# Three chunks per scatter matmul, and the clear of the accumulators on ACT, in a graph attention kernel

## The chip, the cores and the metric

The kernel runs on one core of a Trainium2 chip. The metric is the device time of one execution in microseconds. Three timed executions of the kernel before took 4207.81, 4209.71 and 4210.2 us; the median is 4209.71 us. Engines are named as the profile names them: PE is TensorE's matmul, PEld its weight load, DVE is VectorE, ACT is ScalarE, POOL is GpSimd, SP is SyncE, which here only issues transfers.

## The reference

A graph with 12500 nodes and 412500 edges, sorted by target node. The layer normalises the node features, projects them, weighs every edge by a softmax over the edges of its target, and adds up the source rows:

```python
h = relu(layernorm(x)) @ W_node.T            # (12500, 4 heads, 32)
e = edge_features @ W_edge.T                 # (412500, 4, 32)
att = leaky_relu(sum(concat([h[src], h[tgt], e]) * a, -1), 0.2)
m = maximum(segment_max(att, tgt), 0)
ex = exp(att - m[tgt])
denom = segment_sum(ex, tgt) + (E - deg)[:, None] * exp(-m)
out = x + segment_sum((ex / denom[tgt])[..., None] * h[src], tgt)
```

## The kernel before, in words

**Preparation.** All nodes are normalised and projected first. The 98 blocks of 128 nodes go in groups of up to nine blocks, and these in units of three: measure takes the statistics (bn_stats, on DVE), root and deviate turn them into scale and shift (ACT, DVE), normalize writes hn (two blocks on ACT, one on DVE), turn transposes it on PE into PSUM (pt) and lets DVE write the rectified copy hT, project multiplies by the weights, keep_rows copies to SBUF on ACT, and write stores a finished group into the table in HBM. The loop runs a counter k: iteration k projects unit k, normalizes and turns unit k + 2 and measures unit k + 6. The order in the code is the order on each engine. The accumulator acc (128 x 392 x 35 numbers) is cleared by a GpSimd memset before the loop (L329). After the loop the extents of the chunks are found (L220 to L223).

**Main loop.** A chunk is 896 edges, seven tiles of 128; a batch is eight chunks, and there are 58 batches, the last with five chunks of which the last holds three tiles. Iteration b of the loop works on two batches at once. For batch b + 1 load fetches the edge features and gather fetches one table row per edge: one indirect DMA per tile, 56 for a full batch, all issued by GpSimd (L481). The gathered rows (hs) have two buffers, so gather of batch b + 1 may start only when the scatter of batch b - 1 has read the same buffer. That is done by a gate: ACT copies a column of the finished sums into a tile sums (L579), and GpSimd copies it into gate (L479) before its first gather. For batch b, weigh computes the attention on DVE and ACT, scatter multiplies the rows by it on DVE (L562) and adds them up per target on PE (L569), and collect copies the sums from PSUM to a tile r on ACT (L591; in the last batch every other copy is made by DVE, L589). begin makes the logits z of batch b + 1 (L499, L502, on PE) and its memberships hot (L518, on DVE). After every second batch, and after each of the last two, merge combines the chunks (L598 to L629) and adds them to acc (L638); finish divides a group of blocks, adds x and writes the output.

**Scatter.** The 896 edges of a chunk reach at most 32 target rows, so a tile's membership is a 128 x 32 matrix of zeros and ones. It is the stationary operand; the 128 x 140 weighted rows (four heads of 35) are the moving one. G is 4: chunk q accumulates in column group q mod 4 of the PE array and the same partitions of PSUM, with a tile position of its own. Two chunks are multiplied and added at a time, their tiles in turns. All is in float32, and each matmul of the program is two PE instructions. Memberships are in tiles of 14 edge tiles, four buffers in turn.

Of the kernel before, what the change touches and what calls it, by code (L numbers as in the profile page):

```python
# [9 lines left out]
F32 = mybir.dt.float32  # L10
# [3 lines left out]
OP = mybir.AluOpType  # L14
# [3 lines left out]
P = 128  # L18
# [18 lines left out]
MB = 2  # L37
MC = MB * CB
W = 32
G = P // W  # L40
NB = -(-N // P)
NQ = NB * (P // W)
GB = 7
# [19 lines left out]
def merges():  # L63

    pairs = [(b, b + MB - 1) for b in range(0, NBT - MB, MB)]
    return pairs + [(b, b) for b in range(len(pairs) * MB, NBT)]


def parts():
# [20 lines left out]
def kernel(  # L90
# [57 lines left out]
    twb = const.tile([P, 2, 2, R], F32, name="twb")  # L148
    nc.gpsimd.memset(twb, 0.0)
    gate = const.tile([P, 1], F32, name="gate")  # L150
    sums = const.tile([P, 1], F32, name="sums")
    carry_m = const.tile([P, 1], F32, name="carry_m")
    nc.gpsimd.memset(carry_m, 0.0)
    carry = const.tile([P, AW - 1], F32, name="carry")
# [13 lines left out]
    with (  # L168
# [124 lines left out]
        def turn(u):  # L293
            pt = pps.tile([P, XS, P], F32, name="pt")
            for i in range(u.m):
                nc.tensor.transpose(pt[:, i, :], u.hn[:, i, :], ident)
            u.hT = p2.tile([P, XS, P], F32, name="hT", bufs=3)
            nc.vector.tensor_scalar(u.hT[:, :u.m, :], pt[:, :u.m, :], 0.0, None, op0=OP.max)

        def project(u):  # L300
            u.ph = pps.tile([P, XS, ROW], F32, name="ph")
# [24 lines left out]

        for _ in range(4):
            load_next()
        nc.gpsimd.memset(acc, 0.0)  # L329
        ahead = 6  # L330
        for u in units[:ahead - 2]:
            for s in rooted:
# [19 lines left out]
        while k < len(units):  # L352
            for s in rooted:
                deviate(s)
            rooted.clear()
            if 0 <= k:
                project(units[k])
            if k + 2 < len(units):
                normalize(units[k + 2])
            for s in measured:  # L360
                root(s)
            measured.clear()
            if full:
                write(full)
            if k + 2 < len(units):
                turn(units[k + 2])
                u = units[k + 2]
                if u is u.s.units[-1]:
                    load_next()
            full = keep_rows(units[k]) if 0 <= k else None  # L370
            if k + ahead < len(units):
                measure(units[k + ahead])
            if k == 4:
                early = [index(b) for b in range(2)]
                load_extents()
            if k % 4 == 0 and 0 <= k // 4 - 4 < NG:
                find_rise(k // 4 - 4)
            k += 1
# [64 lines left out]
    em_ps = bank[:, T * R + W:]  # L443
    nc.scalar.copy(rows_ps, riota)

    class Batch:
        pass

# [27 lines left out]
    def gather(s, sums=None):  # L476

        if sums is not None:
            nc.gpsimd.tensor_copy(gate, sums)  # L479
        for i in s.tiles:  # L480
            nc.gpsimd.indirect_dma_start(  # L481
                out=s.hs[:, i, :], out_offset=None, in_=table[:, :],
                in_offset=bass.IndirectOffsetOnAxis(ap=s.src[:, i:i + 1], axis=0))
# [6 lines left out]
    def begin(s):  # L490

        for k in range(2):
            pair = 2 * s.b + k
            nc.vector.tensor_scalar(s.mem[:, k, :], s.mem[:, k, :].bitcast(I32), nid[:, pair:pair + 1], None,  # L494
                                    op0=OP.is_equal)
        s.z = ps.tile([R, CE], F32, name="z")
        for part in (slice(0, HALF), slice(HALF, CE)):
            for j in range(SB):
                nc.tensor.matmul(s.z[:, part], wa3[:, j, :], s.eft[:, j, part], start=(j == 0), stop=False)  # L499
        for part in (slice(0, HALF), slice(HALF, CE)):  # L500
            for k in range(2):
# [10 lines left out]
        s.hot = []  # L512
        for j in range(SB):
            sc = s.b * SB + j
            if not tiles_of(sc):
                continue
            hot = work.tile([P, CT, W], F32, name="hot", bufs=4)
            nc.vector.tensor_tensor(hot, rows_ps[:, None, :].to_broadcast([P, CT, W]),  # L518
                                    key[:, j * CT:(j + 1) * CT, None].to_broadcast([P, CT, W]),
                                    op=OP.is_equal)  # L520
            s.hot.append(hot)

    def weigh(s):

# [27 lines left out]

    def scatter(s):

        s.pa = ps.tile([P, CB // G, H * AW], F32, name="pa", bufs=2)
        by_chunk = s.hs[:, :, :EROW].rearrange("p (q t) (h k) -> p q t h k", t=T, h=H)
        for j in range(SB):
            tiles = list(enumerate(tiles_of(s.b * SB + j)))
            for c, n in tiles:
                q = 2 * j + c  # L560
                rows = by_chunk[:, q, :n, :, :HB]
                nc.vector.tensor_tensor(  # L562
                    rows, rows, ex_ps[:, :n, q * H:(q + 1) * H, None].to_broadcast([P, n, H, HB]), op=OP.mult)
            for i in range(T):
                for c, n in tiles:
                    if i < n:
                        q = 2 * j + c
                        g = q % G
                        nc.tensor.matmul(s.pa[g * W:(g + 1) * W, q // G, :], s.hot[j][:, c * T + i, :],  # L569
                                         s.hs[:, q * T + i, :EROW],  # L570
                                         start=(i == 0), stop=(i == n - 1), tile_position=(0, g * W))

    merged = {}

    def collect(s, first, n):


        if s.b + 2 < NBT:
            nc.scalar.copy(sums, s.pa[:, CB // G - 1, 0:1])  # L579
        if s.b == first:  # L580
            r = work.tile([P, AW * (MC + 1)], F32, name="r")
            merged["r"] = r[:, :AW * (n + 1)].rearrange("p (d c) -> p d c", d=AW)
        at = 1 + (s.b - first) * CB
        for g in range(min(s.chunks, G)):
            to = merged["r"][:, :, at + g:at + s.chunks:G]
            for h in range(H):
                what = s.pa[g * W:(g + 1) * W, :-(-(s.chunks - g) // G), h * AW:(h + 1) * AW]
                if s.b == NBT - 1 and h % 2:
                    nc.vector.tensor_copy(to[h * W:(h + 1) * W, :, :], what.rearrange("p c d -> p d c"))  # L589
                else:  # L590
                    nc.scalar.copy(to[h * W:(h + 1) * W, :, :], what.rearrange("p c d -> p d c"))  # L591

    def merge(c0, n):

# [132 lines left out]
    with tc.manual_schedule():  # L727
        for b in range(-1, NBT):
            if b == -1:
                for k in range(2):  # L730
                    batch(k).src, batch(k).dst = early[k]
                load_pen(batch(0))
            elif b + 2 < NBT:
                batch(b + 2).src, batch(b + 2).dst = index(b + 2)
            if b + 1 < NBT:
                load(batch(b + 1))
                gather(batch(b + 1), sums if b >= 1 else None)
            if b >= 0:
                s = batch(b)
                weigh(s)  # L740
                if b + 1 < NBT:
                    load_pen(batch(b + 1))
                for store in stores:
                    store()
                stores.clear()
                scatter(s)
            if b + 1 < NBT:
                begin(batch(b + 1))
            if b >= 0:
                first, last = next((i, j) for i, j in merges() if i <= b <= j)  # L750
                n = min((last + 1) * CB, NCH) - first * CB
                collect(batch(b), first, n)
                if b == last:
                    merge(first * CB, n)
# [259 lines left out]
```

## Time and profile before

| what | value |
|---|---|
| median of the timed executions | 4209.71 us |
| profiled execution, own time | 5270.07 us |
| profiled execution, span | 5268.3 us |
| TensorE clock granted, mean | 0.599 |
| POOL busy | 3102.0 us, 59% |
| DVE busy | 1776.6 us, 34% |
| PE busy | 1494.8 us, 28% |
| ACT busy | 500.8 us, 10% |
| first gather issued | 111.46 us |
| last gather issued | 5182.26 us |

The profiled execution is much longer than the timed ones, so a share of its span is not a share of the median. In a row of a group the numbers after the bar are busy time in us, the mean of one instruction in ns, and the time that the engine stood idle just before them, with what ended most of it. In a row of the waits the numbers are the sum in us, the count, and the longest. In the timeline they are start and length in us; "x8" means eight instructions drawn together.

### The profile page before, as it was taken

To read this page: it belongs to the slowest core of one execution; us is meant where nothing else is said; L and a number is where in the kernel's file an instruction comes from. 1 tells how busy PE (TensorE), PEld (TensorE's weight loads), DVE (VectorE), ACT (ScalarE), POOL (GpSimd) and SP (SyncE) were. 2 spreads that over 40 slices of the span, in tenths; PEclk is the share of its full clock that TensorE was granted. 3 is DMA by queue.
4 is the path that set the end of the run, shared out by engine and by line. 5 is a ranking of instruction groups with operands and counts; after the bars stand their busy time and mean duration, and the time that the engine had idled before them with its cause. 6 is when DMAs were issued, how large, how long until landed. Compare 5 with 4: busy or idle time off the path is not lost.

```text
span 5268.3 us, 30111 instructions
## 1 busy us (share of the span) xinstructions
PE 1494.8 (28%) x8641; PEld 736.7 (14%) x8641; DVE 1776.6 (34%) x3342; ACT 500.8 (10%) x1629; POOL 3102.0 (59%) x3338
## 2 busy tenths in 40 slices
PE   5232213322323132223232322232323223322223
PEld 4011101111111011111110111111111111111111
DVE  7132424242234142332331432423223324242235
ACT  3010101010001010100010100000101001000001
POOL 3766656556656656565566464655665656555652
PEclk7565656565656565656565655565656656555656
DMA  4332323232323232223232232332232323232321
GB/s 139 100 91 70 112 67 95 73 93 72 96 72 94 70 92 78 84 79 93 72 89 80 81 86 68 94 90 75 83 86 66 101 66 96 75 90 69 98 70 47
DMA packets 243648, 441.28 MB, mean 84 GB/s; under 512 B 93946, under 2 KB 144118, under 8 KB 243478
## 3 DMA queue, kind: packets, MB, share of 16 engines
q0 software_dynamic: 103136, 237.83, 17.7%
q1 hardware_dynamic: 127030, 194.11, 10.7%
q10 hardware_dynamic: 13312, 7.36, 0.5%
q8 instruction: 72, 1.18, 0.1%
q14 instruction: 98, 0.80, 0.0%
HBM read 423.75 MB, written 15.29 MB: 83 GB/s over the span
## 4 chain that ended last, share of the span: by engine, by line
issue 34%; POOL 22%; another core or an unknown queue 15%; PE 12%; DVE 11%; DMA 3%; ACT 2%; DVEq 0%; SPq 0%; ACTq 0%; POOLq 0%
POOL hs L481 22%; PE pa L569 10%; DVE hs L562 2%; DMA hs<-table,src 2%; ACT r L591 1%; PE z L499 1%; DVE up L539 1%; DVE m L541 1%; DMA twb<-table 1%; DVE z L535 1%; DVE acc L638 1%; ACT a L536 1%; DVE a L542 0%; ACT both L545 0%
## 5 line engine op out<-in xcount | busy, mean ns | idle before, releaser
L481 POOL DMA_INDIRECT hs<-table,src x3223 | 3064.6, 951 | 1009.4 <-issue 969.1
L569 PE MATMUL pa<-hs,hot 128*32 128x140 f32 x6446 | 875.0, 397 | 3515.6 <-issue 1754.9
L569 PEld LDWEIGHTS pa<-hs,hot 128*32 128x32 f32 x6446 | 515.1, 151 | 3896.6 <-issue 2021.8
L518 DVE TENSOR_TENSOR hot<-exr,key 128x448 f32<-128x448 f32 x231 | 140.1, 623 | 1940.3 <-remote 1193.2
L479 POOL COPY gate<-sums 128x1 f32<-128x1 f32 x56 | 10.2, 183 | 992.0 <-ACT sums L579 992.0
L562 DVE TENSOR_TENSOR hs<-hs,exr 128x924 f32<-128x924 f32 x461 | 476.8, 1102 | 0.0
L499 PE MATMUL z<-eft,wa 128*32 128x384 f32 (+1 forms) x928 | 373.6, 557 | 22.0 <-issue 22.0
L708 DVE TENSOR_TENSOR xg<-up,xg 128x448 f32<-128x448 f32 (+2 forms) x30 | 16.4, 589 | 771.4 <-remote 767.6
L579 ACT COPY sums<-pa 128x1 f32<-128x1 f32 x56 | 8.9, 159 | 2777.8 <-PE pa L569 2777.8
L591 ACT COPY r<-pa 32x70 f32<-32x70 f32 (+1 forms) x920 | 250.7, 272 | 31.8 <-PE pa L569 19.8
L536 ACT ACTIVATE a<-z 32x224 f32<-32x224 f32 x232 | 80.5, 347 | 1329.1 <-DVE z L535 1079.2
L502 PE MATMUL z<-mem,twb 128*32 128x512 f32 x464 | 186.5, 545 | 5.1 <-DMA twb<-table 5.1
L535 DVE TENSOR_TENSOR z<-z,zst 32x224 f32<-32x224 f32 x232 | 89.8, 387 | 277.4 <-PE z L502 151.4
L499 PEld LDWEIGHTS z<-eft,wa 128*32 128x32 f32 x928 | 99.9, 113 | 238.9 <-issue 234.4
L545 ACT ACTIVATE both<-a 32x224 f32<-32x224 f32 x232 | 89.9, 388 | 370.9 <-DVE a L542 257.1
L638 DVE TENSOR_TENSOR acc<-acc,a 128x70 f32 x461 | 110.0, 239 | 32.9 <-issue 16.5
L539 DVE TENSOR_TENSOR_SCAN up<-pen,z 32x896 f32<-32x896 f32 x58 | 117.0, 2017 | 2.0
L541 DVE TENSOR_TENSOR_SCAN m<-pen,up 32x896 f32<-32x896 f32 x58 | 116.4, 2007 | 2.0
L547 DVE SCALAR_TENSOR_TENSOR both<-pen,m 32x224 f32<-32x224 f32 x232 | 88.0, 380 | 17.8 <-issue 15.7
L703 PE MATMUL up<-a,ident 128*32 128x224 f32 (+2 forms) x480 | 45.2, 554 | 146.6 <-issue 120.5
L494 DVE TENSOR_SCALAR mem<-mem,nid 128x896 f32<-128x896 int32 x116 | 73.9, 677 | 22.7 <-DMA mem<-in_dstc 17.6
L537 DVE TENSOR_TENSOR z<-z,a 32x896 f32<-32x896 f32 x58 | 63.0, 1087 | 24.5 <-issue 15.8
(139 smaller groups left out, 867.8 us busy)
## 6 DMA issues: line engine op xcount, KB each, us to landing
eft<-in_ef SPq DMA_DIRECT2D x58, 1792.0 KB
mem<-in_dstc SPq DMA_DIRECT2D x116, 448.0 KB
hs<-table,src POOLq DMA_INDIRECT x3223
twb<-table SPq DMA_DIRECT2D x464, 0.5 KB
pen<-pens SPq DMA_DIRECT2D x58, 112.1 KB
xg<-in_x SPq DMA_DIRECT2D x14, 448.0 KB
table<-rows ACTq DMA_DIRECT2D x9, 648.0 KB
out<-xg SPq DMA_DIRECT2D x13, 448.0 KB
```

Of the source, the lines that this page charges most:

```text
L481: nc.gpsimd.indirect_dma_start(out=s.hs[:, i, :], out_offset=None, in_=table[:, :], in_offset=bass.IndirectOffsetOnAxis(ap=s.src[:, i:i + ...
L499: nc.tensor.matmul(s.z[:, part], wa3[:, j, :], s.eft[:, j, part], start=(j == 0), stop=False)
L502: nc.tensor.matmul(s.z[:, part], twb[:, s.b % 2, k, :], s.mem[:, k, part], start=False, stop=(k == 1))
L518: nc.vector.tensor_tensor(hot, rows_ps[:, None, :].to_broadcast([P, CT, W]), key[:, j * CT:(j + 1) * CT, None].to_broadcast([P, CT, W]), o ...
L535: nc.vector.tensor_tensor(grouped(s.z, g), grouped(s.z, g), zst[g * R:(g + 1) * R, :, :], op=OP.add)
L536: nc.scalar.activation(grouped(att, g), grouped(s.z, g), AF.Identity, scale=0.2)
L539: nc.vector.tensor_tensor_scan(up, s.pen[:, :CE], s.z, 0.0, op0=OP.add, op1=OP.max)
L541: nc.vector.tensor_tensor_scan(m[:, ::-1], s.pen[:, CE:0:-1], up[:, ::-1], 0.0, op0=OP.add, op1=OP.max)
L562: nc.vector.tensor_tensor(rows, rows, ex_ps[:, :n, q * H:(q + 1) * H, None].to_broadcast([P, n, H, HB]), op=OP.mult)
L569: nc.tensor.matmul(s.pa[g * W:(g + 1) * W, q // G, :], s.hot[j][:, c * T + i, :], s.hs[:, q * T + i, :EROW], start=(i == 0), stop=(i == n ...
L591: nc.scalar.copy(to[h * W:(h + 1) * W, :, :], what.rearrange("p c d -> p d c"))
L638: nc.vector.tensor_tensor(cols, cols, put[:, i0 + i, :, :], op=OP.add)
```

## The change

The group size G becomes 3. The memberships of a batch lie in one tile ordered by tile, then chunk, then row, so that those of three neighbouring chunks form one 128 x 96 stationary operand. The moving operand is the weighted rows of the same three chunks, 128 x 420. The product has nine blocks of 32 x 140, of which the three on the diagonal are kept. A full batch is three groups of chunks (three, three and two); the last batch goes chunk by chunk. Each group has a PSUM tile of its own, in two buffers, and collect is called after each group: it copies 32 x 35 pieces, one per chunk and head. The copy for the gate follows the last group.

The clear of acc moves from a GpSimd memset ahead of the preparation to a copy of a zero column on ACT behind it. And the rectified copy hT leaves turn: it becomes keep_turned, which comes after measure in the same iteration.

```diff
-G = P // W
+G = 3
...
-            u.hT = p2.tile([P, XS, P], F32, name="hT", bufs=3)
-            nc.vector.tensor_scalar(u.hT[:, :u.m, :], pt[:, :u.m, :], 0.0, None, op0=OP.max)
+            u.pt = pt
+
+        def keep_turned(u):
+            u.hT = p2.tile([P, XS, P], F32, name="hT", bufs=3)
+            nc.vector.tensor_scalar(u.hT[:, :u.m, :], u.pt[:, :u.m, :], 0.0, None, op0=OP.max)
...
-        nc.gpsimd.memset(acc, 0.0)
...
                 measure(units[k + ahead])
+            if k + 2 < len(units):
+                keep_turned(units[k + 2])
...
+    hot = work.tile([P, T, CB, W], F32, name="hot")
...
-            hot = work.tile([P, CT, W], F32, name="hot", bufs=4)
-            nc.vector.tensor_tensor(hot, rows_ps[:, None, :].to_broadcast([P, CT, W]),
-                                    key[:, j * CT:(j + 1) * CT, None].to_broadcast([P, CT, W]),
-                                    op=OP.is_equal)
-            s.hot.append(hot)
+        for q0 in range(0, s.chunks, 2):
+            k = key[:, q0 * T:q0 * T + CT].rearrange("p (q t) -> p q t", t=T)
+            nc.vector.tensor_tensor(hot[:, :, q0:q0 + 2, :].rearrange("p t q r -> p q t r"),
+                                    rows_ps[:, None, None, :].to_broadcast([P, 2, T, W]),
+                                    k[:, :, :, None].to_broadcast([P, 2, T, W]), op=OP.is_equal)
...
+        step = G if s.b + 1 < NBT else 1
+        for q0 in range(0, s.chunks, step):
+            w = min(step, s.chunks - q0)
+            for q in range(q0, q0 + w):
...
                 nc.vector.tensor_tensor(
                     rows, rows, ex_ps[:, :n, q * H:(q + 1) * H, None].to_broadcast([P, n, H, HB]), op=OP.mult)
...
-                        nc.tensor.matmul(s.pa[g * W:(g + 1) * W, q // G, :], s.hot[j][:, c * T + i, :],
-                                         s.hs[:, q * T + i, :EROW],
-                                         start=(i == 0), stop=(i == n - 1), tile_position=(0, g * W))
+            pa = ps.tile([P, G * H * AW], F32, name="pa", bufs=2)
...
+            for i in order:
+                v = w if i < n else w - 1
+                nc.tensor.matmul(pa[:v * W, :v * H * AW], hot[:, i, q0:q0 + v, :].rearrange("p q r -> p (q r)"), by_chunk[:, q0:q0 + v, i, :],
+                                 start=(i == order[0]), stop=(i == order[-1]))
+            collect(s, q0, w, pa)
...
-        if s.b + 2 < NBT:
-            nc.scalar.copy(sums, s.pa[:, CB // G - 1, 0:1])
+        if s.b + 2 < NBT and q0 + w == s.chunks:
+            nc.scalar.copy(sums, pa[:W, 0:1])
...
+        for q in range(w):
+            at = 1 + (s.b - first) * CB + q0 + q
             for h in range(H):
+                to = merged["r"][h * W:(h + 1) * W, :, at]
+                k = (q * H + h) * AW
+                if s.b == NBT - 1 and q0 + w == s.chunks and h % 2:
+                    nc.vector.tensor_copy(to, pa[q * W:(q + 1) * W, k:k + AW])
                 else:
+                    nc.scalar.copy(to, pa[q * W:(q + 1) * W, k:k + AW])
...
             if b == -1:
+                nc.scalar.copy(acc.rearrange("p q d -> p (q d)"), carry_m.to_broadcast([P, NQ * AW]))
```

More of the change, by code (lines that the diff above doesn't have):

```diff
@@ L66, in merges, with merge_of, chunks_of @@
     return pairs + [(b, b) for b in range(len(pairs) * MB, NBT)]
+def merge_of(b):
+    return next((i, j) for i, j in merges() if i <= b <= j)
+def chunks_of(first, last):
+    return min((last + 1) * CB, NCH) - first * CB
 def parts():
@@ L150 @@
     gate = const.tile([P, 1], F32, name="gate")
-    sums = const.tile([P, 1], F32, name="sums")
+    sums = const.tile([W, 1], F32, name="sums")
     carry_m = const.tile([P, 1], F32, name="carry_m")
@@ L478, in gather @@
         if sums is not None:
-            nc.gpsimd.tensor_copy(gate, sums)
+            nc.gpsimd.tensor_copy(gate[:W, :], sums)
         for i in s.tiles:
@@ L511, in begin @@
         nc.vector.tensor_tensor(key, key, dk, op=OP.add)
[L512 to L516, printed above, removed]
-            hot = work.tile([P, CT, W], F32, name="hot", bufs=4)
-            nc.vector.tensor_tensor(hot, rows_ps[:, None, :].to_broadcast([P, CT, W]),
-                                    key[:, j * CT:(j + 1) * CT, None].to_broadcast([P, CT, W]),
-                                    op=OP.is_equal)
-            s.hot.append(hot)
+        for q0 in range(0, s.chunks, 2):
[3 more added lines that the diff above has]
+                                    k[:, :, :, None].to_broadcast([P, 2, T, W]), op=OP.is_equal)
     def weigh(s):
@@ L553, in scatter @@
     def scatter(s):
[L555 to L561, printed above, removed]
+        by_chunk = s.hs[:, :, :EROW].rearrange("p (q t) k -> p q t k", t=T)
+        held = [n for j in range(SB) for n in tiles_of(s.b * SB + j)]
@@ L562, in scatter @@
+        step = G if s.b + 1 < NBT else 1
+        for q0 in range(0, s.chunks, step):
+            w = min(step, s.chunks - q0)
+            for q in range(q0, q0 + w):
+                n = held[q]
+                rows = by_chunk[:, q, :n, :].rearrange("p t (h k) -> p t h k", h=H)[:, :, :, :HB]
                 nc.vector.tensor_tensor(
                     rows, rows, ex_ps[:, :n, q * H:(q + 1) * H, None].to_broadcast([P, n, H, HB]), op=OP.mult)
[L564 to L569, printed above, removed]
-                                         s.hs[:, q * T + i, :EROW],
-                                         start=(i == 0), stop=(i == n - 1), tile_position=(0, g * W))
@@ L573 @@
-    merged = {}
-    def collect(s, first, n):
-        if s.b + 2 < NBT:
-            nc.scalar.copy(sums, s.pa[:, CB // G - 1, 0:1])
-        if s.b == first:
+            pa = ps.tile([P, G * H * AW], F32, name="pa", bufs=2)
+            n = held[q0 + w - 1]
+            order = [0, *range(n, T if w > 1 else n), *range(1, n)]
+            for i in order:
+                v = w if i < n else w - 1
+                nc.tensor.matmul(pa[:v * W, :v * H * AW], hot[:, i, q0:q0 + v, :].rearrange("p q r -> p (q r)"), by_chunk[:, q0:q0 + v, i, :],
+                                 start=(i == order[0]), stop=(i == order[-1]))
@@ L581, in collect @@
+            collect(s, q0, w, pa)
+    merged = {}
+    def collect(s, q0, w, pa):
+        first, last = merge_of(s.b)
+        if s.b + 2 < NBT and q0 + w == s.chunks:
+            nc.scalar.copy(sums, pa[:W, 0:1])
+        if s.b == first and q0 == 0:
+            n = chunks_of(first, last)
             r = work.tile([P, AW * (MC + 1)], F32, name="r")
             merged["r"] = r[:, :AW * (n + 1)].rearrange("p (d c) -> p d c", d=AW)
-        at = 1 + (s.b - first) * CB
-        for g in range(min(s.chunks, G)):
-            to = merged["r"][:, :, at + g:at + s.chunks:G]
+        for q in range(w):
+            at = 1 + (s.b - first) * CB + q0 + q
@@ L586, in collect @@
             for h in range(H):
-                what = s.pa[g * W:(g + 1) * W, :-(-(s.chunks - g) // G), h * AW:(h + 1) * AW]
-                if s.b == NBT - 1 and h % 2:
-                    nc.vector.tensor_copy(to[h * W:(h + 1) * W, :, :], what.rearrange("p c d -> p d c"))
+                to = merged["r"][h * W:(h + 1) * W, :, at]
+                k = (q * H + h) * AW
+                if s.b == NBT - 1 and q0 + w == s.chunks and h % 2:
+                    nc.vector.tensor_copy(to, pa[q * W:(q + 1) * W, k:k + AW])
@@ L590, in collect @@
                 else:
-                    nc.scalar.copy(to[h * W:(h + 1) * W, :, :], what.rearrange("p c d -> p d c"))
+                    nc.scalar.copy(to, pa[q * W:(q + 1) * W, k:k + AW])
     def merge(c0, n):
@@ L749 @@
             if b >= 0:
-                first, last = next((i, j) for i, j in merges() if i <= b <= j)
-                n = min((last + 1) * CB, NCH) - first * CB
-                collect(batch(b), first, n)
+                first, last = merge_of(b)
                 if b == last:
-                    merge(first * CB, n)
+                    merge(first * CB, chunks_of(first, last))
                 del batches[b]
```

## The prediction

> **What bounds the kernel now.** I read the start of the trace first, then the groups, the waits, one steady batch and the last two batches. The span is 5268.3 us, the profiled execution's own time 5270.07 us, but the three timed runs have a median of 4209.71 us. That gap of 1060 us decides what may be read from this profile, so it comes first. From the page's groups and the waits:
>
> ```profile
> span 5268.3 us, 30111 instructions
> L481 POOL DMA_INDIRECT hs<-table,src x3223 | 3064.6, 951 | 1009.4 <-issue 969.1
> L479 POOL COPY gate<-sums 128x1 f32<-128x1 f32 x56 | 10.2, 183 | 992.0 <-ACT sums L579 992.0
> L569 PE MATMUL pa<-hs,hot 128*32 128x140 f32 x6446 | 875.0, 397 | 3515.6 <-issue 1754.9
> L562 DVE TENSOR_TENSOR hs<-hs,exr 128x924 f32<-128x924 f32 x461 | 476.8, 1102 | 0.0
> ```
>
> GpSimd issues 3223 gathers at (3064.6 + 969.1) / 3223 = 1.25 us each, 70 us for a full batch of 56. It stands still for anything else only at the 56 gates, 992.0 us in sum. The gate of batch b+1 waits for the scatter of batch b-1. Why is that late here? The timeline of one steady batch:
>
> ```profile
> 2606.45 0.95 POOL L481 DMA_INDIRECT hs<-table,src  x1 [0.30 <-issue]
> 2607.21 0.39 PE L569 MATMUL pa<-hs,hot 128*32 128x140 f32 x1 [2.47 <-issue]
> 2608.61 0.13 PEld L569 LDWEIGHTS pa<-hs,hot 128*32 128x32 f32 x1 [2.67 <-issue]
> 2610.01 0.39 PE L569 MATMUL pa<-hs,hot 128*32 128x140 f32 x1 [2.41 <-issue]
> ```
>
> While gathers are being issued TensorE falls, after some 42 scatter matmuls, to one instruction (load or matmul) per 1.4 us, with nothing that the profile shows to wait for; once the gathers of that batch are out, the rest runs at 0.1 us. Is that so in an untraced run? Add up without it: 5268.3 - 992.0 = 4276. Without gate waits batch 56 also starts while the last 31 gathers are still going out instead of 3 us before their end, about 33 us earlier: 4243, which is 0.8% over the median. With the stalls the sum is 25% over. I take it that the timed runs have almost no gate wait: **they are first gather + 3223 x 1.25 us + the end**, and the stalls of TensorE belong to the traced execution. Here a rule of the Trainium skill speaks otherwise (Runtime: NRT & Kernel Launch, section on the preamble and postamble): a profile's total is about 6 us above the reported time whatever the kernel. By that rule the 992 us would be real and fewer matmuls a large gain (the third rival); this case's pair, 5270 against 4209.7, contradicts it, and the measurement decides.
>
> So only three stretches can move the median: what lies before the first gather (111.46 us), the cadence of the gathers, and what follows the last full gather. The start, from the timeline, then the two engines' mutual wait in the preparation:
>
> ```profile
> 2.33 11.57 DVE L187 CAST prf<-pr 128x2 f32<-128x2 int32 x1
> 2.34 11.53 POOL L329 MEMSET acc<- 128x13720 f32 x1
> 14.27 0.67 DVE L255 BATCH_NORM_STATS2 stats<-xg 128x6 f32<-128x128 f32 x3
> ...
> 111.46 1.12 POOL L481 DMA_INDIRECT hs<-table,src  x1 [4.60 <-DVE ext L222]
> ```
>
> ```profile
> DVE hT L298 <- PE pt L296: 24.3, 33, 1.4
> PE pt L296 <- ACT hn L290: 11.6, 10, 2.1
> PE pt L296 <- DVE hn L287: 11.0, 15, 1.3
> ```
>
> A cast of two elements per partition lasts 11.57 us, exactly as long as the GpSimd memset beside it; everything of VectorE queues behind it. And the end:
>
> ```profile
> 5200.19 8.29 DVE L562 TENSOR_TENSOR hs<-hs,exr 128x924 f32<-128x924 f32 x8
> 5210.42 4.62 ACT L591 COPY r<-pa 32x70 f32<-32x70 f32 x16 [11.15 <-PE pa L569]
> 5215.07 0.17 DVE L603 TENSOR_SCALAR mc<-r 128x8 f32<-128x8 f32 x1 [2.77 <-ACT r L591]
> 5239.78 4.65 DVE L562 TENSOR_TENSOR hs<-hs,exr 128x924 f32<-128x924 f32 x5
> 5241.96 5.49 PE L569 MATMUL pa<-hs,hot 128*32 128x140 f32 x60 [0.35 <-DVE hs L562]
> 5251.29 0.22 DVE L589 COPY r<-pa 32x35 f32<-32x35 f32 x1 [0.28 <-ACT r L591]
> ```
>
> **The change, part by part.**
>
> *The clear of acc leaves GpSimd.* The cast then ends at about 2.5 us, and the statistics wait for their rows. No row has that landing; the matmul on the first weights starts at 3.54 us, and the DMA engines have moved about half a megabyte by 4 us, where the first rows are 192 KB. So the statistics start near 4.3 instead of 14.27 us: **-10 us**, and all that follows is a chain from there (the loads of the next groups are finished by 9 us, before they are wanted). Ends: -11.5 (the memset's length) and 0 (the cast is long for another reason). The ACT copy that replaces it: 128x528 takes 0.61 us and 128x16 0.22 us, 0.76 ns an element, so 13720 take 10.5 us. On ACT it stands behind the copy of riota (120.80 us); ACT's next work is weigh of batch 0 after some 70 us of gathers. Nothing; without that cover 10.5 us.
>
> *The rectified copy (hT) goes behind the statistics of a later unit.* In the preparation VectorE waits 24.3 us for transposes and TensorE 22.6 us for hn, 33 units long: each turns the other round. Now 0.59 us of statistics fill each wait. The waits recur as 0.42, 0.57, 0.69 and 1.31 us, of which 0.42, 0.57, 0.59 and 0.59 are covered, 0.54 on average, 18 us in all at most. It is 0 at least, if TensorE becomes the bound: from 20 to 108 us it is busy 62.1 of 88 us, 1.88 us a unit, against a period now of 2.6 (roots at 44.03 and 90.82 us, six groups of three units apart) and 2.06 with the whole gain; ACT is at 1.38. There is room, but with nothing to spare when the clock falls (granted 0.54 from 44 to 52 us). I take two thirds: **-12 us**. What is late next is hT by 0.6 us, wanted by project two iterations later. Loads and table writes then ask for more than the 158 GB/s of 52 to 76 us, while 36 to 44 us show 331.
>
> *Scatter.* Per full batch 112 matmuls of 140 columns become 42 of 420, 420 and 280: the same 15680 columns, with the loads 96 wide. Price of a column: the loads of L499 follow each other at 0.43 us for 512 columns and 0.32 for 384, 0.84 ns a column with no remainder for the load, so 14 x 0.353 + 14 x 0.353 + 14 x 0.235 = 13.2 us. Before, four column groups of the array overlapped, and 84 went at 0.071 us, VectorE's pace. The rule here (TensorE: Matmul & The Clock Gate, Part 3) is against the change twice: column packing, which it gives up, is worth 2.38x for three tiles, and a weight load hides behind a matmul only in another row group. By the price of a load in its section LDWEIGHTS (columns / 1.2, an estimate of 80 ns for 96) the 42 would take 3.4 us more. L499, always in the same rows, shows the load hidden; I keep 13.2 us.
>
> In the steady state this is covered by GpSimd. One batch's chain with 16 chunks merged and a finish: z to the next transposition is 39.2 us in batch 56 (5187.79 to 5226.97), plus 5.9 for the longer merge, 3 for landing, now some 4 to 6 more: 54 against 70. The gate's own need, the end of scatter, comes about 32 us into the gather. **0**; if the cover were gone, each us per batch costs 58. The memberships in one tile (four writes of 0.62 us) now surely wait for the last matmul; also covered. The copies become 32 of 35 columns instead of 16 of 70, most while TensorE works on. The gathers' cadence: the VectorE work beside them is the same, 0.
>
> *The end.* Batch 56, multiplications from 5200.19: three chunks ready at 5203.3, TensorE to 5208.3, 5213.2, 5216.5; eight copies of 0.25 to 5218.8: merge 3.8 us later. Batch 57 goes chunk by chunk: 62 matmuls in one column group at 0.12 to 0.14 us end near 5249, 1.5 us later, but only the last chunk's four copies follow instead of sixteen (4.0 us): -1.4. **+2.4 us**; ends -1 (the copies alone) and +16 (loads exposed at half clock).
>
> Sum: -10 - 12 + 2.4 = -19.6, on its own time 5270.07 apart from the gates, and on the median **4190 us**.
>
> **Rivals.** (1) *No change.* TensorE bounds the preparation at once and the end takes the weight loads: -10 + 0 + 8 gives 4208. For: 1.88 us is a mean at a clock that varies. Against: its 22.6 us of waits. (2) *The cast was not held by the memset*: -12 + 2.4, 4200. Against: 11.53 and 11.57. (3) *The stalls are real in timed runs.* Then a gather costs (4209.7 - 111 - 992 - 85 - 46) / 3223 = 0.92 us, and 289 TensorE instructions a batch become 149. At 0.71 per us during 70 us 50 get through; now 239 are left for 18.5 us (12.9 per us), then 99, in 7.7: gates down by 10 us each, 560 in all: 3650. (4) *Slower.* The new scatter outlasts the cover: place the gate and the wait for landing, price 58 us per us. Two batches leave some 60 us free, so it decides when a matmul takes over (13.2 + 30) / 42 = 1.03 us, three times L499's price: with 1.05 us, 4240. For it only the rule on packing.
>
> **How the numbers follow.** 0.2%, 8.4 us, is about what a measurement of this kernel can tell from no change. Chances: forecast 0.62, (1) 0.17, (2) 0.09, (3) 0.05, (4) 0.07. The range takes the forecast's bounds and the first two rivals, 4174 to 4214; outside are (3), (4) and some 0.07 of the edges. Faster: most of the forecast (0.6), (3), and half of (2) with a little of (1), 0.72; slower: (4) and the end at +16 with little gained ahead, 0.10; the rest 0.18.
>
> **What will show it.** The cast at 0.2 us and statistics near 4.3 us; the root every 6.2 us instead of 7.8; the first gather at 87 to 95 us; 2456 scatter matmuls at about 0.35 us; gathers at 1.25 us. The profiled span should fall far more than the median, to some 4700 us, as gates wait less: if the median falls with it, (3) was right. I am wrong if the gathers' cadence changes, or if the first gather stays above 100 us.

## The result and the profile after

Twenty runs of the changed kernel have a median of 4203.4 us (4201.13 to 4206.4), twenty of the kernel before 4209.84 us (4205.96 to 4212.01). The ratio is 0.9985, with a 95% interval of 0.9979 to 0.9992: 6.4 us less (3.4 to 8.8), where 20 were forecast.

One thing about the comparison first. The profile of before came from an execution of 5270 us, in which TensorE is held up: for long stretches it gets one instruction done per 1.4 us. The profile of after took 4203.49 us, as its timed runs do, and its gates wait for nothing. All experiments below ran on four chips, their traces show TensorE held up as in the profile of before, and there the kernel before takes 5268 to 5304 us in its timed runs too. So two kinds of execution are met, and the prediction's reading that the stalls come with tracing is wrong. Below they are called executions with and without hold-ups; whether it is the chip that decides between them was not shown. For differences of a few us the two profiles are compared stretch by stretch, before the first gather and behind the multiplications of the last two batches, not by their spans.

From the profile of after, its span, the gathers, the gates, the scatter's matmuls and the copies behind them:

```profile
span 4201.7 us, 23990 instructions
L497 POOL DMA_INDIRECT hs<-table,src x3223 | 3073.3, 954 | 978.2 <-issue 968.1
L495 POOL COPY gate<-sums 32x1 f32<-32x1 f32 x56 | 10.9, 195 | 0.3
L583 PE MATMUL pa<-hs,hot 128*96 128x420 f32 (+2 forms) x2456 | 902.1, 531 | 2465.3 <-issue 2421.5
L606 ACT COPY r<-pa 32x35 f32<-32x35 f32 x1842 | 385.3, 209 | 819.0 <-PE pa L583 799.1
```

GpSimd issues a gather every (3073.3 + 968.1) / 3223 = 1.25 us, as before, and its 56 gates (L495) waited 0.3 us in sum, against 992.0 in the profile of before. So the time is first gather + gathers + end, and each of the three can be read. The start, from the timeline of after:

```profile
2.32 0.17 DVE L197 CAST prf<-pr 128x2 f32<-128x2 int32 x1
2.66 1.28 ACT L745 ACT_TABLE_LOAD   x1 [2.66 <-issue]
3.72 0.68 DVE L265 BATCH_NORM_STATS2 stats<-xg 128x6 f32<-128x128 f32 x3 [0.76 <-DMA xg<-in_x]
3.95 11.62 ACT L745 COPY acc<-carry_m 128x13720 f32<-128x13720 f32 x1
15.59 1.28 ACT L282 ACT_TABLE_LOAD   x1
16.89 0.30 ACT L282 ACTIVATE rstd<-dif,eps 128x3 f32<-128x3 f32 x1
17.22 0.18 DVE L287 RECIPROCAL rstd<-rstd 128x3 f32<-128x3 f32 x1 [12.15 <-ACT rstd L282]
...
95.19 1.12 POOL L497 DMA_INDIRECT hs<-table,src  x1 [4.60 <-DVE ext L232]
104.51 0.19 ACT L458 COPY exr<-riota 128x32 f32<-128x32 f32 x1 [14.10 <-DVE off L415]
```

The cast takes 0.17 us and the statistics start at 3.72 us, as forecast. But the new copy that clears acc runs at 3.95 us, ahead of the first square root of the preparation. Nothing but a table load precedes it on ACT, although the file has it behind the whole preparation and behind the copy of riota, which runs at 104.51 us. The square root waits for it and begins at 16.89 us; in the profile of before it began at 16.99:

```profile
16.99 0.30 ACT L272 ACTIVATE rstd<-dif,eps 128x3 f32<-128x3 f32 x1
```

VectorE now waits 12.15 us for the square root. The chain that ended last has the copy as one of its longest pieces:

```profile
3.95 11.62 ACT acc L745
```

The waits between 2 and 108 us (us in total, times, longest) show the other step of the preparation:

```profile
DVE rstd L287 <- ACT rstd L282: 12.5, 2, 12.2
DVE hT L311 <- PE pt L306: 7.7, 13, 1.1
PE pt L306 <- ACT hn L300: 7.3, 8, 1.7
PE pt L306 <- DVE hn L297: 7.1, 10, 2.0
```

VectorE's wait for the transposes fell from 24.3 to 7.7 us, TensorE's for hn from 22.6 to 14.4. The first gather moved from 111.46 to 95.19 us. The end, from the timeline of the last two batches of after (zst is the transposition with which a batch's attention starts):

```profile
4128.57 8.28 DVE L575 TENSOR_TENSOR hs<-hs,exr 128x924 f32<-128x924 f32 x8
4131.92 14.99 PE L583 MATMUL pa<-hs,hot 128*96 128x420 f32 x42 [45.34 <-issue]
4148.75 0.17 DVE L618 TENSOR_SCALAR mc<-r 128x8 f32<-128x8 f32 x1 [3.94 <-ACT r L606]
4159.72 0.57 DVE L538 STREAM_TRANSPOSE zst<-hs 128x224 f32<-128x224 f32 x1
4172.53 4.65 DVE L575 TENSOR_TENSOR hs<-hs,exr 128x924 f32<-128x924 f32 x5
4173.73 10.24 PE L583 MATMUL pa<-hs,hot 128*32 128x140 f32 x62 [14.88 <-issue]
```

From the multiplications of batch 56 to the next batch's transposition it is 31.15 us, where before had 26.78, from 5200.19 to this line of its timeline:

```profile
5226.97 0.57 DVE L527 STREAM_TRANSPOSE zst<-hs 128x224 f32<-128x224 f32 x1
```

That is 4.4 us more. From the multiplications of batch 57 to the end of the span it is 29.2 us against 28.5.

### The profile page after: what moved, and what is told of

The parts are those of the page before. It is cut to its first block, busy times and chain, and to the rows that moved or that the text cites. A ratio compares the mean times of both kernels' runs of the same rounds, so it can differ in the third digit from the quotient of the medians.

```text
span 4201.7 us, 23990 instructions
## 1 busy us (share of the span) xinstructions
PE 1537.7 (37%) x4651; PEld 630.5 (15%) x4651; DVE 1767.9 (42%) x3336; ACT 648.3 (15%) x2553; POOL 3099.8 (74%) x3337
## 3 DMA queue, kind: packets, MB, share of 16 engines
q1 hardware_dynamic: 127030, 194.11, 13.8%
## 4 chain that ended last, share of the span: by engine, by line
POOL 71%; issue 24%; DVE 2%; DMA 1%; PE 1%; ACT 1%; SPq 0%; POOLq 0%; ACTq 0%; DVEq 0%
POOL hs L497 71%; DMA hs<-table,src 1%; PE pa L583 1%; DVE hT L311 0%; ACT acc L745 0%; DVE stats L265 0%; POOL gate L495 0%; DVE hn L297 0%; PE pt L306 0%; ACT hn L300 0%; PE ph L316 0%; DMA twb<-table 0%; DVE acc L653 0%; DVE tot L271 0%; ACT r L606 0%
## 5 line engine op out<-in xcount | busy, mean ns | idle before, releaser
L497 POOL DMA_INDIRECT hs<-table,src x3223 | 3073.3, 954 | 978.2 <-issue 968.1
L583 PE MATMUL pa<-hs,hot 128*96 128x420 f32 (+2 forms) x2456 | 902.1, 531 | 2465.3 <-issue 2421.5
L583 PEld LDWEIGHTS pa<-hs,hot 128*96 128x96 f32 (+2 forms) x2456 | 413.7, 173 | 2965.6 <-issue 2829.1
L538 DVE STREAM_TRANSPOSE zst<-hs 128x224 f32<-128x224 f32 x58 | 33.6, 579 | 1681.2 <-DMA hs<-table,src 1681.2
L606 ACT COPY r<-pa 32x35 f32<-32x35 f32 x1842 | 385.3, 209 | 819.0 <-PE pa L583 799.1
L515 PE MATMUL z<-eft,wa 128*32 128x384 f32 (+1 forms) x928 | 361.5, 543 | 21.2 <-DMA twb<-table 21.2
L510 DVE TENSOR_SCALAR mem<-mem,nid 128x896 f32<-128x896 int32 x116 | 73.3, 672 | 21.5 <-DMA mem<-in_dstc 21.5
L518 PEld LDWEIGHTS z<-mem,twb 128*32 128x32 f32 x464 | 51.2, 111 | 130.9 <-issue 114.3
L553 DVE TENSOR_TENSOR a<-z,m 32x896 f32<-32x896 f32 x58 | 62.5, 1078 | 2.0
```

Source lines behind the costliest of these rows:

```text
L497: nc.gpsimd.indirect_dma_start(out=s.hs[:, i, :], out_offset=None, in_=table[:, :], in_offset=bass.IndirectOffsetOnAxis(ap=s.src[:, i:i + ...
L583: nc.tensor.matmul(pa[:v * W, :v * H * AW], hot[:, i, q0:q0 + v, :].rearrange("p q r -> p (q r)"), by_chunk[:, q0:q0 + v, i, :], start=(i ...
L606: nc.scalar.copy(to, pa[q * W:(q + 1) * W, k:k + AW])
```

## The experiments

The theory after the result: the clear moved its 11.6 us from VectorE's path to ACT's and gained nothing; hT alone made the start shorter; the merged scatter costs some 5 us at the end, and nothing among the gathers where they are the bound. The rivals: the clear still gains and hT gains less; the matmuls decide wherever gates wait, which is rival (3) of the prediction.

Most expectations give two numbers, for a chip without hold-ups and for one with them. All runs met hold-ups, so the first of the two could never be tested.

Times are medians of timed runs in us, "before" being the kernel before on the same chip; kernels that share a value of before ran on one chip. The last two columns are from the traces, in us: when the first gather is issued, and the sum of the waits of the 56 gates.

| kernel | us | before | ratio, 95% interval | first gather | gate waits |
|---|---|---|---|---|---|
| e1 hT alone | 5289.1 | 5303.8 | 0.9974 [0.9965, 0.9983] | 96.20 | 1030.6 |
| e2 clear alone | 5303.1 | 5303.8 | 1.0001 [0.9992, 1.0009] | 110.66 | 1030.5 |
| e3 scatter alone | 5208.2 | 5303.8 | 0.9829 [0.9814, 0.9843] | 109.66 | 933.1 |
| e4 change, clear late | 5188.0 | 5303.8 | 0.9784 [0.9765, 0.9804] | 85.60 | 922.4 |
| e5 scatter alone | 5139.9 | 5267.7 | 0.9757 [0.9737, 0.9777] | 109.80 | 877.5 |
| e6 change, clear late | 5111.2 | 5267.7 | 0.9700 [0.9686, 0.9714] | 87.03 | 845.1 |
| e7 hT and late clear | 5245.6 | 5267.7 | 0.9957 [0.9943, 0.9971] | 86.47 | 1003.8 |
| e8 late clear alone | 5261.5 | 5267.7 | 0.9986 [0.9972, 1.0000] | 100.25 | 1003.3 |
| e9 the change | 5154.2 | 5272.1 | 0.9786 [0.9764, 0.9808] | 95.91 | 879.6 |
| e10 change, clear late, old end | 5141.1 | 5272.1 | 0.9752 [0.9739, 0.9766] | 87.14 | 874.0 |
| e11 before, 3 tiles of 7 | 5081.5 | 5272.1 | 0.9638 [0.9624, 0.9651] | 109.47 | 808.8 |
| e12 scatter alone | 5164.6 | 5272.1 | 0.9786 [0.9770, 0.9802] | 111.04 | 904.4 |
| e13 change, clear late, old end | 5097.1 | 5271.0 | 0.9668 [0.9655, 0.9681] | 85.77 | 884.3 |
| e14 change, clear late | 5116.9 | 5271.0 | 0.9708 [0.9695, 0.9721] | 86.05 | 869.7 |
| e15 scatter alone | 5123.4 | 5271.0 | 0.9732 [0.9712, 0.9751] | 111.10 | 837.4 |

**The clear alone, where the change puts it (e2).** On the kernel before:

```diff
-        nc.gpsimd.memset(acc, 0.0)
...
             if b == -1:
+                nc.scalar.copy(acc.rearrange("p q d -> p (q d)"), carry_m.to_broadcast([P, NQ * AW]))
```

> The kernel before with only the clear of acc moved to ACT, written where the change writes it. Theory: the copy of 11.6 us comes to stand at the head of ACT's queue and holds the first square root exactly as the memset held the first cast, so the first gather stays at 111.4 us and the time at 4209.8, within 2 us. Rival (the prediction): 10 us less, 4200.

No difference could be measured. The timeline shows why; the lines are its cast, first statistics, copy and first square root:

```profile
2.32 0.17 DVE L187 CAST prf<-pr 128x2 f32<-128x2 int32 x1
3.92 0.68 DVE L255 BATCH_NORM_STATS2 stats<-xg 128x6 f32<-128x128 f32 x3 [0.96 <-DMA xg<-in_x]
3.96 11.62 ACT L729 COPY acc<-carry_m 128x13720 f32<-128x13720 f32 x1
16.89 0.30 ACT L272 ACTIVATE rstd<-dif,eps 128x3 f32<-128x3 f32 x1
```

The statistics are 10.3 us earlier than with the memset and the square root is where it was. The hold was moved, not removed.

**The clear after the preparation (e4, e6, e14 with the change; e8 alone; e7 with hT).** The same copy is written as the last ACT work of the preparation:

```diff
             if k + 2 < len(units):
                 keep_turned(units[k + 2])
...
+        nc.scalar.copy(acc.rearrange("p q d -> p (q d)"), carry_m.to_broadcast([P, NQ * AW]))
...
             if b == -1:
-                nc.scalar.copy(acc.rearrange("p q d -> p (q d)"), carry_m.to_broadcast([P, NQ * AW]))
```

Expected of e4:

> The changed kernel with the clear of acc written at the end of the preparation, so that on ACT it follows the last copy of the projected rows. Theory: the 11.6 us then lie beside the gathers of batch 0, where ACT has nothing to do; statistics and first square root move up by 10 us, the first gather to 85 us, the time from 4203.4 to 4193. Rival (the preparation is bound by the loads of the rows once it starts earlier): less than 4 us of it arrive, 4200.

Expected of e6:

> The changed kernel with the late clear once more, for a chip without hold-ups. Theory: 10 us under the changed kernel's 4203.4, so 4193; rival (the loads bound the preparation): 4200. With hold-ups: 116 us under the kernel before, as in the fourth experiment.

Expected of e8:

> The kernel before with only the late clear of acc on ACT. Theory: the memset did hold the first cast and all behind it, so the first gather comes 10 us earlier, near 101 us, and the time falls by 10 us (4200 without hold-ups). Rival (the preparation's loads, or the mutual waits of VectorE and TensorE, swallow the earlier start): less than 4 us.

Expected of e7:

> The kernel before, its scatter in four column groups untouched, with the later rectified copy and the late clear. Theory: it keeps the whole gain of the start (first gather at 85 us, 26 us less) and has none of the longer end, so without hold-ups 4184, which is 9 to 10 us under the changed kernel with the late clear; with hold-ups about 26 us under the kernel before, and 90 us over the changed kernel with the late clear. Rival (the merged scatter has no cost in the end beside this): within 3 us of the sixth run without hold-ups.

Expected of e14:

> The change with the clear late in the preparation. On a chip that does not hold TensorE up: 4193 to 4194 us, 9.6 us under the changed kernel, since the first gather starts by that much earlier and the gathers set the time. On one that does: 0.970 to 0.978.

Square root and copy in the timeline of e14:

```profile
6.55 0.30 ACT L282 ACTIVATE rstd<-dif,eps 128x3 f32<-128x3 f32 x1
81.90 11.62 ACT L394 COPY acc<-carry_m 128x13720 f32<-128x13720 f32 x1 [0.62 <-POOL rows L324]
```

The square root comes 10.3 us earlier than in after. The first gather is at 85.6 to 87.0 us in e4, e6 and e14 against 95.2 and 95.9 in the two traces of the change (after and e9), 9.3 us earlier on average; without hT and without the merged scatter (e8) it is at 100.25 against 109.80 in e5, on the same chip. So the forecast's 10 us are there to be had at the first gather, if the copy waits its turn. In the times they do not stand out cleanly: e8 gained 6.2 us, with an interval that reaches no change, and on the chips of e4, e6 and e14 the change itself was not run. e7 gained 22.1 us, where 26 were expected.

These runs also narrow down why the copy of the change ran early. It has the same operands in both places. In the kernel the preparation and the main loop are two blocks (`tc.manual_schedule()`). Written in the block of the main loop, the copy runs ahead of all ACT work of the preparation; written at the end of the preparation's block, it runs there. So that it depends on nothing is not enough to bring it to the head. What puts an instruction of the second block ahead of the first was not found.

**hT alone (e1).** The helper keep_turned and its call, nothing else of the change:

```diff
+            u.pt = pt
+
+        def keep_turned(u):
             u.hT = p2.tile([P, XS, P], F32, name="hT", bufs=3)
...
+            if k + 2 < len(units):
+                keep_turned(units[k + 2])
```

> The kernel before with only the later rectified copy (hT behind the statistics). Theory: the whole gain of the changed kernel's start is this edit, so the first gather comes at 95 us instead of 111.5 and the time falls by 16 us to about 4194. Rival (the prediction's own split: 12 us here, 10 from the clear): the first gather at 99.5 us and 4198. Rival (TensorE becomes the bound without the other edits): less than 5 us.

It gained 14.7 us (9 to 19); its first gather is 14.5 us earlier than that of e2 on the same chip, and e7's is 13.8 us earlier than e8's. As the clear by itself gained nothing (e2), this part made nearly all of the 16.3 us by which the first gather moved.

**The merged scatter alone (e3, e5, e12, e15).** The one-tile hot, the groups of three chunks and their copies; the memset stays and hT is made in turn as before:

```diff
+        step = G if s.b + 1 < NBT else 1
+        for q0 in range(0, s.chunks, step):
...
+                nc.tensor.matmul(pa[:v * W, :v * H * AW], hot[:, i, q0:q0 + v, :].rearrange("p q r -> p (q r)"), by_chunk[:, q0:q0 + v, i, :],
+                                 start=(i == order[0]), stop=(i == order[-1]))
```

Expected of e3:

> The kernel before with only the scatter of three chunks per matmul (and its collect). Theory: nothing in the steady state, and the end longer by what the two traces show, 4.4 us in batch 56 and 0.7 in batch 57: 4215. Rival (the cadence of the gathers suffers from the new scatter as well, which would explain that the measured gain is 5 us smaller than start and end together): 4220, with the gathers' region 5 us longer than the kernel before would have without its stalls. Rival (the merged scatter helps the timed runs): under 4205. All theories: the profiled span falls from 5268 to within 10 us of the timed median, since the traced stalls of TensorE go with the number of its instructions.

Expected of e5:

> The same kernel as the third experiment, in the hope of a chip on which TensorE's completions are not held up (the first four experiments ran on one where the kernel before takes 5304 us). There: start unchanged, end 5 us longer, 4215 if that is all, 4220 if the gathers' cadence suffers too, under 4210 if the merged scatter helps in some way not seen. On a chip with the hold-ups: 95 us less than the kernel before, as in the third experiment.

Expected of e12:

> The merged scatter alone. On a chip that does not hold TensorE up: 5 us slower than before if it costs only at the end, 10 us slower if the gathers also take 5 us longer beside it. On a chip that does: 95 to 130 us faster, as in its other two runs.

Expected of e15:

> The merged scatter alone. On a chip that does not hold TensorE up: 4215 us if it costs only at the end, 4220 us if the gathers also take 5 us longer beside it. On a chip that does: 0.976 to 0.983, as in its other runs.

Where TensorE is held up, this part gains 96 to 148 us, and its gates wait for correspondingly less: e3's 97 us less than e2's on the same chip, for 95.6 us of time. The first gather comes as before (109.66 to 111.10 us). So rival (3) holds on these chips in kind, but not in size: it counted on 560 us. The size was not foreseen either: e5, e6, e13 and e15 gained more than was expected of them, e15 for example 148 us where 0.976 to 0.983 allows 90 to 127. What the merged scatter costs without hold-ups no run of it alone could show, as none was without them.

**The change itself (e9).**

> The changed kernel itself, beside the one before on the same chip. If on this chip the kernel before takes about 4210 us, TensorE is not held up here, and the change should repeat its 6 us: ratio about 0.9985. If the kernel before takes 5250 to 5300 us, it is a chip that holds TensorE up, and the change should give the sum of what its parts gave on such chips: about 95 to 130 us for the scatter, 15 us for hT, nothing for the clear: ratio 0.972 to 0.980. The first gather at about 95 us on either.

117.9 us less than before, which is about the sum of the parts on such chips: 107.5 for the scatter (e12, the same chip), 14.7 for hT (e1), nothing for the clear. The change is thus worth 6 us in the one kind of execution and 118 in the other.

**Fewer matmuls (e11).** The kernel before with the matmuls of the first three tiles of seven; the others are left out:

```diff
-                    if i < n:
+                    if i < min(n, 3):
...
-                                         start=(i == 0), stop=(i == n - 1), tile_position=(0, g * W))
+                                         start=(i == 0), stop=(i == min(n, 3) - 1), tile_position=(0, g * W))
```

> The kernel before with the matmuls of only the first three tiles of a chunk: four sevenths of the scatter's matmuls and of their weight loads are left out, all else is as it was. If the hold-ups of TensorE go with the number of instructions that TensorE completes while GpSimd issues gathers, this removes twice as many of them as the change does per batch for the same time of gathers: on a chip that holds TensorE up the time falls by well over 100 us, towards 4240. If they go with GpSimd's gathers alone, the time stays within 20 us of before. On a chip that does not hold TensorE up: no change, within 0.2%, since TensorE is behind the gathers there.

Per full batch 128 of 289 TensorE instructions (64 matmuls and their loads) are gone, and the time falls by 190.6 us only, not towards 4240; of some 1000 us of gate waits 808.8 stay. The expectation counts wrongly: the change removes 140 instructions (112 matmuls and their loads become 42), so e11 removes slightly fewer, not twice as many, and yet gains more than the 107.5 us of the merged scatter on the same chip (e12). So the number of instructions does not set the hold-up by itself. e11 also drops four sevenths of the columns, which the change keeps; whether that makes the difference was not tested. Lines of its timeline in a steady batch, a load and the next matmul, then the copy that lets the gate go:

```profile
2518.77 0.13 PEld L569 LDWEIGHTS pa<-hs,hot 128*32 128x32 f32 x1 [2.67 <-issue]
2520.17 0.39 PE L569 MATMUL pa<-hs,hot 128*32 128x140 f32 x1 [2.41 <-issue]
...
2561.43 0.16 ACT L579 COPY sums<-pa 128x1 f32<-128x1 f32 x1 [61.09 <-remote]
2561.65 0.18 POOL L479 COPY gate<-sums 128x1 f32<-128x1 f32 x1 [9.42 <-ACT sums L579]
```

One TensorE instruction per 1.4 us, with nothing the profile shows to wait for. The scatter's last matmul ended at 2523.36, yet ACT's copy of its sums starts 38 us later, and 9 us after the last gather of the batch (2551.29 + 0.95). So, as the trace has it, not only is TensorE slow while gathers go out: its completions reach the other engines late, and the gate pays for that lateness.

**The old column groups for the last two batches (e10, e13).** On the change with the late clear:

```diff
-        step = G if s.b + 1 < NBT else 1
+        if s.b + 2 >= NBT:
+            return scatter_packed(s, by_chunk)
+        step = G
```

where scatter_packed is the scatter of before, with four column groups of 32 and the copies of 70 columns behind all of its matmuls.

Expected of e10:

> The change with the clear late in the preparation, and with the four column groups of before in the last two batches alone. If the merged scatter costs time only at the end (4.4 us in batch 56, 0.7 in batch 57), this gains about 5 us over the same kernel with every batch merged, and on a chip that does not hold TensorE up some 14 to 15 us over the changed kernel: about 0.995 of the kernel before. If the scatter also costs 5 us among the gathers (the part of the changed kernel's time that start and end leave unexplained), that 5 us stays, and the ratio is about 0.9950 rather than 0.9938.

Expected of e13:

> The change with the late clear and the column groups of before in the last two batches, once more. On a chip that does not hold TensorE up (kernel before about 4210 us): 4188 us if the merged scatter costs only at the end, 4193 us if 5 us more are lost among the gathers. On a chip that does: 0.970 to 0.976, as in its first run.

The end of batch 56 in the timeline of e10:

```profile
5053.39 8.28 DVE L599 TENSOR_TENSOR hs<-hs,exr 128x924 f32<-128x924 f32 x8
...
5063.62 4.62 ACT L619 COPY r<-pa 32x70 f32<-32x70 f32 x16 [11.15 <-PE pa L606]
5068.27 0.17 DVE L652 TENSOR_SCALAR mc<-r 128x8 f32<-128x8 f32 x1 [2.77 <-ACT r L619]
5080.16 0.57 DVE L539 STREAM_TRANSPOSE zst<-hs 128x224 f32<-128x224 f32 x1
```

From the multiplications to the transposition it is 26.77 us, the 26.78 of before; kernels with the merged scatter have 31.2 to 32.4 in the same place. The old end gives the 4.4 us and more back in the trace. Batch 57 did not gain: 29.4 us to the end of the span, where the merged ones have 28.0 to 29.8 and those with the old scatter throughout 27.2 to 28.5. In the times the two fall by 13.1 us against the change (e9, intervals overlapping) and 19.8 us against the change with the late clear (e14). The 19.8 us are more than the 4.4 that the trace shows at the end, and e13's single runs lie between 5071 and 5129 us; what the rest of them is was not found. It is the fastest complete kernel on both its chips, though its lead over e9 is within their intervals. Without hold-ups 4203.4 - 9.3 - 4.4, about 4190 us, is an estimate from the traces, since no experiment ran without them. The gathers would leave room for the 4.4: in after the last is issued at 4152.28 us, a transposition starts 2.6 us behind the last gather of its batch, and the one at 4159.72 would move to 4155.3.

## Why the prediction was right or wrong

**The step that failed: the clear at "-10 us" with a copy on ACT that costs "Nothing".** Its first half was right: the memset had held the cast (11.57 to 0.17 us), and rival (2) is excluded. What failed is the sentence that on ACT the copy "stands behind the copy of riota". It stood at the head of ACT, at 3.95 us, and the price named "without that cover", 10.5 us, became due as 11.6: 10.6 us gained by VectorE (statistics at 3.72 instead of 14.27), all but 0.1 lost again at the square root. The position in the file was taken for the position on the engine, as the description of the kernel above says of the preparation that "the order in the code is the order on each engine". For this copy, written in the block behind, it is not. It needs only carry_m, which is ready from the start, and nothing of the preparation, so nothing held it back. e2 shows the exchange alone, e4, e6, e8 and e14 the 9 to 10 us with the copy late. So -10 stood in the sum where nothing was gained.

**hT behind the statistics: right in mechanism, a little under-sized.** -12 us stood in the sum, within bounds of -18 and 0; it gave 13.8 to 14.7 us in e1, e7 and e8. The forecast of the root every 6.2 us is met: in after 44.55 to 81.64 us is six groups, 6.2 us each. TensorE did not become the bound (rival 1): the transposes are waited for less than before.

**Scatter in the steady state: right where TensorE runs freely.** The price of a column and the hidden weight loads hold at full clock. Two loads of 96 columns at the start of batch 56 and two further on, in the timeline of after:

```profile
4133.40 0.28 PEld L583 LDWEIGHTS pa<-hs,hot 128*96 128x96 f32 x1 [0.42 <-issue]
4134.10 0.28 PEld L583 LDWEIGHTS pa<-hs,hot 128*96 128x96 f32 x1 [0.42 <-issue]
...
4136.26 0.16 PEld L583 LDWEIGHTS pa<-hs,hot 128*96 128x96 f32 x1 [0.19 <-issue]
4136.61 0.16 PEld L583 LDWEIGHTS pa<-hs,hot 128*96 128x96 f32 x1 [0.19 <-issue]
```

The first two are 0.70 us apart, the later two 0.35, where the granted clock is 1.00 (4135.2 to 4146.9 us). That leaves no room for the 80 ns that the prediction estimated from the Trainium skill (TensorE: Matmul & The Clock Gate, section LDWEIGHTS); the measurement decides against adding it for these shapes. (Its 3.4 us take all 42 loads as 96 wide; 14 are 64 wide, which makes the estimate 3.0.) In after gates wait 0.3 us, so the cover of GpSimd's gathers is there and rival (4) with it excluded.

**The end: +2.4 was +5.0.** Batch 56 gave +4.4 rather than +3.8. Its matmuls took 15.0 us instead of the 13.2 of the cadence alone, as the first few went at 0.70 us, at a granted clock of 0.55 (4131.9 to 4135.2 us); so the merge began 5.3 us later than in before (20.18 us after the multiplications instead of 14.88). 0.9 us came back behind it, where the matmuls of finish ran at a granted clock of 1.00 in after and of 0.50 in before:

```profile
4157.56 1.29 PE L718 MATMUL up<-a,ident 128*32 128x160 f32 x32 [1.51 <-DVE a L711]
```

```profile
5223.74 2.36 PE L703 MATMUL up<-a,ident 128*32 128x160 f32 x32 [4.78 <-DVE a L696]
```

That the sum came near +3.8 is in part luck. Batch 57 gave +0.7 rather than -1.4: its 62 matmuls took 10.24 us, 0.165 each, where 0.12 to 0.14 was taken, at a granted clock of 0.74 between 4172 and 4186 us. Both are inside the bounds given.

**The sum.** -14 to -16 at the start and +5 at the end make -9 to -11; measured is -6.4 (3.4 to 8.8). What is left, some 3 to 5 us at the medians, is open. The gathers' busy time in after is 3073.3 us, 8.7 more than in the profile of before; single ones beside VectorE's work take 1.34 to 1.37 instead of 0.94 us. Of the 64 in after that took more than 1.2 us, 54 lie beside VectorE's making of mem (L510), nearly one per batch. The profile of before has 13 such gathers, 11 of them beside the same work. With hold-ups there are 17 to 27 in the traces with the merged scatter and 3 to 13 in those without, so the merged scatter may have a share in it. Whether the kernel before has as many when its gates don't wait was not seen, since every trace of it comes from an execution with hold-ups.

**Hold-ups "belong to the traced execution": wrong.** That timed runs at 4209.7 us have almost no gate wait fits the trace of after, with 0.3 us of them at 4203.49 us, though the kernel before was never traced in such an execution; so the median was to be judged without them. But they occur in timed runs too, on four chips, and the span of after did not fall "to some 4700" but, on an execution without them, to the median itself; in those with them it is 5138 us (e9), as the scatter gained 96 to 148 us of the 560 that rival (3) counted on. That sum let the backlog run down at a fixed rate for each instruction; e11 shows that most of a gate's wait stays with less than half of the scatter's matmuls. Nor did the pair 5270 and 4209.7 us speak against the rule of the Trainium skill (Runtime: NRT & Kernel Launch, section on the preamble and postamble) that a profile's total is about 6 us above the reported time: the pair compared executions of two kinds. Within one execution the span is 1.8 us below its own time here (5268.3 and 5270.07 us, 4201.7 and 4203.49), which is not the page's 6 us above, but no gap of 1060 either. What makes one execution hold TensorE up and another not was not found.

## What to carry to other kernels

Work that is moved to another engine "where it has time" must be looked up in that engine's order of execution, not in the file: here a copy that nothing held back, written in a later block, ran at the head of its engine and held what was on the path; written at the end of the earlier block, it stayed there. When a hold is removed, read what the next instruction on the path waits for in the new trace before counting the gain. And when profile and timed runs disagree by a quarter, think of two kinds of execution, as there were here, and cost a change under both: the merged scatter, which by the traces is worth nothing or less in one, was worth 1.7 to 2.7% in the other.

## What the runs showed of the hardware

A small VectorE cast beside a GpSimd memset of 128 x 13720 lasts as long as the memset (11.57 and 11.53 us), and 0.17 us without it; beside an ACT copy of the same size, VectorE's statistics take their usual 0.68 us. A matmul with 96 stationary columns and 420 moving ones has a cadence of 0.353 us in the same rows of the array, its load included, at a granted clock of 1.00, and of 0.70 us at 0.55. Indirect gathers beside VectorE's making of mem took 1.34 to 1.37 us on GpSimd instead of 0.94. In executions with hold-ups, TensorE falls to one instruction per 1.4 us while GpSimd issues a gather per 1.25 us, and its completions become visible up to 38 us late (e11); the time of the kernel before is then 5268 to 5304 instead of 4210 us.
